# Staging the end of a second layer by a table of times, with a normalisation's division and weight in one VectorE product

## The chip, the cores and the metric

The kernel runs on one core of a Trainium2 chip. The metric is the device time of one execution in microseconds. The profiler has recorded one further execution; its times are those of the views below. Engines are named as in the profile: PE is TensorE, PEld its weight loads, DVE is VectorE, ACT is ScalarE, POOL is GpSimd, and SP issues the transfers.

## What is computed

The program is a network of four layers on an input of 2 x 56 x 56 tokens of 128 channels. The first two layers are scans in four directions, the third is an attention with a spectral mixer, the fourth an attention with experts. The change lies where the second layer ends and the third begins. For every token, the reference computes there (shortened):

```python
y = _layernorm(y, p['out_norm_w'], p['out_norm_b']) * jax.nn.silu(z)
out = y @ p['out_proj_w'].T                       # for each of four heads of 32 channels
prev = s + out + vss_skip * s                     # the head's block
x_res = cvm_skip * x_orig + jnp.concatenate(outs, axis=3)
x = _layernorm(x_res, final_ln_w, final_ln_b)     # 128 channels
u = _ln_t(x)                                      # a second normalisation, without weight
sim = jnp.einsum('blh,bmh->blm', u, u) * scale    # attention of the third layer
```

## The kernel before

The tokens lie as X, 112 partitions by 28 tiles by 2 images by 128 channels, in SBUF for the whole program. The stage between the last scan and attention 2 runs over seven chunks of four tiles (448 tokens) of both images together. A chunk goes through three bodies, called one after the other in a loop in `Layer1.run` (from L935):

- `after` (L872), for the last head: ScalarE squares y (L881), GpSimd multiplies y with the gate (L883), TensorE projects both and the mean of the squares (L888, L890, L892; the trace shows eight rows for each four matmuls), ScalarE takes the root (L894), VectorE its reciprocal (L895), `u` (L899), `t` (L903) and X (L905), and GpSimd adds to `u` between (L901).
- `last` (L910): the final layernorm of the second layer, in place in X. `layernorm_tokens` (L71) sums on VectorE (L78), scales (L79), subtracts (L80), squares on ScalarE (L81), sums (L82), takes root (L83, ScalarE) and reciprocal (L84), and then, as `last="ACT"`, scales each of the eight rows of 128 channels on ScalarE (L89). Two GpSimd passes over 112x1024 multiply with the weight and add the bias (both L918). Its tiles are called `stf` and `sqf`.
- `Attention2.chunk` (L1133): the second normalisation, of X into U, by the same function (tiles `stu` and `squ`). Then TensorE turns U (L1145), image by image; `evacuate` (L58) copies the result from PSUM to `uT`, a part of `big`, alternating between VectorE (L64) and ScalarE (L68); and `key_tiles` (L1279) turns `uT` back into tiles of keys (L1285), with one or two such copies.

Nothing in this loop fixes the order in which the instructions stand in the engines' queues. The framework's scheduler chooses it, from priorities and readiness, and it also places instructions of neighbouring parts among them: the small ones that form the mixer's weights (L1380 to L1409, L1707 to L1709), and the first score matmuls of attention 2 (L1076). The scans before it run inside `manual_schedule()`, where the order written is the order issued. In either case each engine works off its queue in that order, and an instruction waits until what it reads is there.

Behind the stage, `mixer_filters` clears a tile P (L1340), fills it by a transfer, and adds windows of it into D (L1349); attention 2 begins with scores (L1076) and their exponentials (L1078).

The pools decide how many chunks can be under way: `mid1` has two buffers for each of the tiles of `after` and `last`, `a2u` two for U, `squ` and `stu`, `pmid1` two PSUM tiles, `pa2` four.

Of the kernel before, what the change touches and what calls it, by code (L numbers as in the profile page):

```python
# [17 lines left out]
ALU = mybir.AluOpType  # L18
# [3 lines left out]
B = 2  # L22
HW = 56
L = HW * HW
C = 128
TP = 112
NT = L // TP
CH = 448
NCH = L // CH
# [38 lines left out]
            self.nc.scalar.copy(out, in_)  # L68


def layernorm_tokens(k, out, x, sq, st, d, by=None, last="POOL"):  # L71

    nc = k.nc
    g = x.shape[1]
    mean, var = st[:, 0, :], st[:, 1, :] if by is None else by
    nc.vector.tensor_reduce(mean, x, AX.X, ALU.add)  # L78
    nc.vector.tensor_scalar_mul(mean, mean, 1.0 / d)  # L79
    nc.vector.tensor_tensor(out, x, mean.unsqueeze(2).to_broadcast([TP, g, d]), ALU.subtract)  # L80
    nc.scalar.activation(sq, out, AF.Square)  # L81
    nc.vector.tensor_reduce(var, sq, AX.X, ALU.add)  # L82
    nc.scalar.activation(var, var, AF.Sqrt, bias=k.eps[:TP], scale=1.0 / d)  # L83
    nc.vector.reciprocal(var, var)  # L84
    if last == "POOL":
        nc.gpsimd.tensor_tensor(out, out, var.unsqueeze(2).to_broadcast([TP, g, d]), ALU.mult)
    else:
        for i in range(g):
            nc.scalar.activation(out[:, i], out[:, i], AF.Copy, scale=var[:, i : i + 1])  # L89


def tokens_to_channels(k, pool, dst, src):
# [18 lines left out]
class Scans:  # L111
# [190 lines left out]
    def run(self):  # L302
        with ExitStack() as ctx:
            self.open(ctx)
            with self.k.tc.manual_schedule():
                self.all_steps()
# [437 lines left out]
class Layer1:  # L744
# [79 lines left out]
    def chunk(self, t, c):  # L824
        return t[:, 4 * c : 4 * (c + 1)].rearrange("p j b c -> p (j b) c")
# [4 lines left out]
    def before(self, head, pools, c, pad):  # L830
# [5 lines left out]
        if c < NCH:  # L836
            sv = self.chunk(self.prev, c)
            xs = self.chunk(self.channels(head), c)
            if head == 0:
                nc.vector.tensor_copy(sv, xs)  # L840
            else:
                nc.vector.tensor_tensor(sv, sv, xs, ALU.add)
            nrm = sp.tile([TP, 4, B * D], F32, name="nrm")
            nv = nrm.rearrange("p j (b c) -> p (j b) c", c=D)
            sq = sp.tile([TP, 4 * B, D], F32, name="sq")
            st = sp.tile([TP, 2, 4 * B], F32, name="st")
            layernorm_tokens(k, nv, sv, sq, st, D)
            nc.gpsimd.tensor_scalar(xs, xs, self.R["cvm_skip"], None, ALU.mult)
            nc.gpsimd.tensor_scalar(sv, sv, self.R["vss_skip"], None, ALU.mult)
            pt = pp.tile([2 * D, CH], F32, name="pt")  # L850
            for i in range(4):
                nc.tensor.transpose(pt[:, TP * i : TP * (i + 1)], nrm[:, i], k.ident[:TP, :TP])
            nc.scalar.copy(self.hT[:, cs], pt)
            ps = vp.tile([128, CH], F32, name="pcv")
            nc.tensor.matmul(ps, lhsT=W["in_w"][:, 0, :], rhs=self.hT[:, cs], start=True, stop=True)
            nc.scalar.activation(
                pad[:, 1 + 8 * c : 9 + 8 * c, 1 : 1 + HW], ps.rearrange("p (r w) -> p r w", w=HW),
                AF.Identity, bias=self.inb[:, 0:1],
            )
# [10 lines left out]
            self.scans.first(vp)  # L870

    def after(self, head, pools, c):  # L872

        k, nc, D = self.k, self.k.nc, self.D
        sp, pp = pools
        cs = slice(CH * c, CH * (c + 1))
        y, gate = self.y[:, cs], self.z[:, cs]
        sq = sp.tile([128, CH], F32, name="sq0")  # L880
        nc.scalar.activation(sq, y, AF.Square)  # L881
        yz = sp.tile([128, CH], F32, name="yc0")
        nc.gpsimd.tensor_tensor(yz, y, gate, ALU.mult)  # L883
        p = pp.tile([TP, 2, 4, B * D], F32, name="p")
        pv = pp.tile([TP, 4 * B], F32, name="pv")
        tiles = [slice(TP * i, TP * (i + 1)) for i in range(4)]
        for i, ts in enumerate(tiles):
            nc.tensor.matmul(p[:, 1, i], lhsT=gate[:, ts], rhs=self.outs[1], start=True, stop=True)  # L888
        for i, ts in enumerate(tiles):
            nc.tensor.matmul(pv[:, B * i : B * (i + 1)], lhsT=sq[:, ts], rhs=self.mean, start=True, stop=True)  # L890
        for i, ts in enumerate(tiles):
            nc.tensor.matmul(p[:, 0, i], lhsT=yz[:, ts], rhs=self.outs[0], start=True, stop=True)  # L892
        rs = sp.tile([TP, 4 * B], F32, name="rs")
        nc.scalar.activation(rs, pv, AF.Sqrt, bias=k.eps[:TP])  # L894
        nc.vector.reciprocal(rs, rs)  # L895
        p1, p2 = (p[:, i].rearrange("p j (b c) -> p (j b) c", c=D) for i in range(2))
        s, x = self.chunk(self.prev, c), self.chunk(self.channels(head), c)
        u = sp.tile([TP, 4 * B, D], F32, name="u")
        nc.vector.tensor_tensor(u, p2, s, ALU.add)  # L899
        if head == 3:  # L900
            nc.gpsimd.tensor_tensor(u, u, x, ALU.add)  # L901
        t = sp.tile([TP, 4 * B, D], F32, name="t")
        nc.vector.tensor_tensor(t, p1, rs.unsqueeze(2).to_broadcast([TP, 4 * B, D]), ALU.mult)  # L903
        if head == 3:
            nc.vector.tensor_tensor(x, t, u, ALU.add)  # L905
        else:
            nc.vector.tensor_tensor(s, t, u, ALU.add)
            nc.gpsimd.tensor_tensor(x, x, s, ALU.add)

    def last(self, sp, c):  # L910

        k, nc = self.k, self.k.nc
        xv = self.chunk(k.X, c)
        sq = sp.tile([TP, 4 * B, C], F32, name="sqf")
        st = sp.tile([TP, 2, 4 * B], F32, name="stf")
        layernorm_tokens(k, xv, xv, sq, st, C, last="ACT")
        for op, n in ((ALU.mult, "final_ln_w"), (ALU.add, "final_ln_b")):
            nc.gpsimd.tensor_tensor(xv, xv, self.R[n].unsqueeze(1).to_broadcast([TP, 4 * B, C]), op)  # L918

    def opened(self, ctx):  # L920
        k, name = self.k, "mid1"
# [13 lines left out]
    def run(self, follow):  # L935


        k = self.k
        for head in range(1, 5):
            self.scans.run()  # L940
            with ExitStack() as ctx:
                pp = ctx.enter_context(k.pool("pmid1", 2, psum=True))
                if head < 4:
                    pad = self.opened(ctx)
                    sp = self.sp
                else:
                    sp = ctx.enter_context(k.pool("mid1", 2))
                    chunk = follow(ctx)
                for c in range(NCH + 1):
                    if c < NCH:  # L950
                        self.after(head - 1, (sp, pp), c)
                    if head < 4:
                        self.before(head, (sp, pp, self.vp), c, pad)
                    elif c < NCH:
                        self.last(sp, c)
                        chunk(c)

# [6 lines left out]
def bank(pool, name):  # L966
    return pool.tile([128, 512], F32, name=name)
# [150 lines left out]
class Attention2:  # L1118
# [14 lines left out]
    def chunk(self, c):  # L1133

        k, nc = self.k, self.k.nc
        U = self.sp.tile([TP, 4, B, C], F32, name="U")
        sq = self.sp.tile([TP, 4 * B, C], F32, name="squ")
        st = self.sp.tile([TP, 2, 4 * B], F32, name="stu")
        flat = "p j b c -> p (j b) c"
        x = k.X[:, 4 * c : 4 * (c + 1)].rearrange(flat)  # L1140
        layernorm_tokens(k, U.rearrange(flat), x, sq, st, C, last="ACT")
        for b in range(B):
            pt = bank(self.pp, "pt")[:, 0:CH]
            for i in range(4):
                nc.tensor.transpose(pt[:, TP * i : TP * (i + 1)], U[:, i, b, :], k.ident[:TP, :TP])  # L1145
            k.evacuate(self.uT[b][:, CH * c : CH * (c + 1)], pt)
            key_tiles(k, bank(self.pp, "pt"), self.uT[b], self.V[b], c)

    def run(self, early, inputs):
# [129 lines left out]
def key_tiles(k, ps, uT, V, c):  # L1279

    j0, j1 = CH * c // KT, NKT if c == NCH - 1 else CH * (c + 1) // KT
    ps = ps.rearrange("p (j c) -> p j c", c=C)
    for j in range(j0, j1):
        t = uT[:, KT * j : min(KT * (j + 1), L)]
        k.nc.tensor.transpose(ps[: t.shape[-1], j - j0, :], t, k.ident)  # L1285
    whole = min(j1, L // KT)
    k.evacuate(V[:, j0:whole], ps[:, 0 : whole - j0])
    if whole < j1:
        n = L - KT * whole
        k.evacuate(V[:n, whole], ps[:n, whole - j0])  # L1290
# [168 lines left out]
class Mixer:  # L1459
# [104 lines left out]
    def into(self, by, place, onto=None):  # L1564
# [3 lines left out]
        for outs in sorted(by, key=len):  # L1568
            ps = self.product(by[outs])
            for o in outs:  # L1570
# [4 lines left out]
                else:  # L1575
                    nc.vector.tensor_tensor(place(o), onto(o), ps, ALU.add)

    def unit(self, f0, eo, after, later, project):


# [463 lines left out]
```

## Time and profile before

| what | value |
|---|---|
| median of three runs | 9114.81 us (9106.39 to 9117.84) |
| the profiled execution | 9098.37 us |
| its span, first to last instruction | 9096.6 us |
| busy over the span: PE | 7993.2 us (88%) |
| busy over the span: DVE | 7088.0 us (78%) |
| busy over the span: POOL | 6350.1 us (70%) |
| busy over the span: ACT | 3854.8 us (42%) |
| mean granted TensorE clock | 0.951 |

The span is what the timeline's times count from. The busy shares are means over parts of the program with quite different limits; the stage of the change is about 120 us of the 9096.6. A row of the timeline gives the start, the time until its last instruction's end, engine, line, operation, what is written from what, the shape and how many instructions were merged; in brackets stands the engine's idle time before it and what ended that. Rows of the same stage by form give busy time and mean duration, then the idle time of the engine before them.

### The profile page before, as it was taken

The numbers are of one execution on the slowest core, as the hardware profiler recorded it, in microseconds if no ns is written. First come the engines' busy times: TensorE is split into PE (matmuls) and PEld (weight loads), VectorE is DVE, ScalarE is ACT, GpSimd is POOL, SyncE is SP. The second block draws the span as 40 slices with busy tenths as digits, with TensorE's granted clock in tenths as the row PEclk, the third lists the DMA queues.
The fourth block names the chain that finished last, engine by engine and source line by source line (L and its number), as shares of the span: only waits on it lengthen the run. The fifth ranks groups of instructions, "written<-read, shape, count | busy, mean of one in ns | idle before, by whom it ended". The sixth has DMA issues, their size and how long they took to land. (4 is left out here: it accounts for less than half of the span.)

```text
span 9096.6 us, 93496 instructions
## 1 busy us (share of the span) xinstructions
PE 7993.2 (88%) x28687; PEld 4765.5 (52%) x28687; DVE 7088.0 (78%) x7568; ACT 3854.8 (42%) x6644; POOL 6350.1 (70%) x4066
## 2 busy tenths in 40 slices
PE   8888888888887888888888888699999999999998
PEld 4444445444444444444444444355688888874555
DVE  8999998999997997998999899511467667665442
ACT  4555545555555555554554555433211111114331
POOL 6999996999996997998899799566311111115551
PEclk9999999999999998998999899799999999999999
DMA  5666664666664995996898699100233333320004
GB/s 159 221 221 220 222 212 127 221 221 220 222 220 110 230 226 134 227 228 157 203 227 204 157 227 224 39 3 3 85 96 105 104 94 110 93 63 8 14 1 135
DMA packets 780368, 1362.92 MB, mean 150 GB/s; under 512 B 133101, under 2 KB 405486, under 8 KB 779834
## 3 DMA queue, kind: packets, MB, share of 16 engines
q1 hardware_dynamic: 779866, 1356.95, 53.1%
q8 instruction: 227, 3.72, 0.2%
q14 instruction: 275, 2.25, 0.1%
HBM read 1317.03 MB, written 39.60 MB: 149 GB/s over the span
## 5 line engine op out<-in xcount | busy, mean ns | idle before, releaser
L430 POOL TENSOR_TENSOR p<-h,c 128x784 f32<-128x784 f32 x2048 | 3761.2, 1864 | 115.0 <-DVE h L358 33.1
L358 DVE TENSOR_TENSOR_SCAN h<-a,state,h 128x784 f32<-128x784 f32 x1536 | 2791.8, 1840 | 51.6 <-ACT a L339 28.7
L378 PE MATMUL acc<-p,center 128*128 128x392 f32 x4096 | 1499.0, 499 | 22.7 <-POOL p L430 20.8
L378 PE MATMUL acc<-p,ident 128*128 128x392 f32 x4096 | 1491.9, 498 | 6.7 <-POOL p L430 6.7
L417 DVE TENSOR_TENSOR h<-du,b 128x784 f32<-128x784 f32 x1408 | 1336.7, 949 | 75.6 <-PE b L364 70.4
L339 ACT ACTIVATE a<-delta,L0A 128x784 f32<-128x784 f32 x1024 | 939.3, 918 | 973.4 <-DVE h L358 971.5
L339 ACT ACTIVATE a<-delta,L1A 128x784 f32<-128x784 f32 x1024 | 939.2, 917 | 908.3 <-DVE h L358 905.3
L364 PE MATMUL b<-three,sel 96*128 96x512 bf16 (+1 forms) x2816 | 728.6, 341 | 563.9 <-DVE h L417 460.1
L433 POOL TENSOR_TENSOR h<-du,b 128x784 f32<-128x784 f32 x640 | 1190.3, 1860 | 4.1 <-PE pcv L460 4.1
L378 PEld LDWEIGHTS acc<-p,center 128*128 128x128 f32 x4096 | 740.9, 192 | 536.8 <-POOL p L430 60.2
L378 PEld LDWEIGHTS acc<-p,ident 128*128 128x128 f32 x4096 | 743.9, 192 | 512.8 <-POOL p L430 26.5
L1089 POOL TENSOR_TENSOR total<-total,e 128x448 f32<-128x448 f32 (+1 forms) x644 | 735.6, 1142 | 326.0 <-ACT e L1078 286.0
L358 DVE TENSOR_TENSOR_SCAN h<-a,h 128x784 f32<-128x784 f32 x512 | 901.7, 1780 | 36.7 <-ACT a L339 21.1
L364 PEld LDWEIGHTS <-sel 96*128 96x128 bf16 x2816 | 281.5, 100 | 1230.9 <-issue 1048.6
L1572 DVE TENSOR_TENSOR u<-u,cv 128x512 f32<-128x512 f32 x1024 | 623.7, 681 | 326.6 <-PE cv L1559 325.4
L1603 POOL TENSOR_TENSOR u<-u,S 128x1024 f32<-128x1024 f32 x64 | 150.0, 2365 | 1041.0 <-DVE S L1572 1041.0
L1078 ACT ACTIVATE e<-sc 128x448 f32<-128x448 f32 (+1 forms) x700 | 377.2, 543 | 723.0 <-PE sc L1076 596.3
L1574 ACT COPY u<-cv 128x512 f32<-128x512 f32 x256 | 149.5, 587 | 829.3 <-PE cv L1559 775.7
L1673 PE MATMUL pj<-u,Wm 128*128 128x196 f32 (+8 forms) x1536 | 354.7, 384 | 5.7 <-DVE A L1679 5.7
L1076 PE MATMUL sc<-big 128*128 128x448 f32 (+1 forms) x700 | 323.4, 547 | 15.4 <-ACT e L1078 12.3
L1070 PE MATMUL av<-e,big 128*128 128x448 f32 (+1 forms) x700 | 320.9, 545 | 1.2 <-DVE e L1083 1.0
L1653 POOL TENSOR_TENSOR both<-mpm 128x512 f32<-128x512 f32 x32 | 40.6, 1269 | 392.3 <-DVE Wm L1709 272.8
(452 smaller groups left out, 11251.1 us busy)
## 6 DMA issues: line engine op xcount, KB each, us to landing
c<-rows SPq DMA_DIRECT2D x1024, 392.0 KB, 4.0
c<-rows SPq DMA_DIRECT2D x2048, 196.0 KB, 4.8
b<-rows SPq DMA_DIRECT2D x320, 392.0 KB, 4.5
b<-rows SPq DMA_DIRECT2D x640, 196.0 KB, 4.6
H<-raw SPq DMA_DIRECT2D x32, 1568.0 KB, 7.6
wC<-win SPq DMA_DIRECT2D x64, 576.0 KB, 6.4
w<-in_L_weight_dram SPq DMA_DIRECT2D x52, 512.0 KB, 6.3
wA<-win SPq DMA_DIRECT2D x64, 384.0 KB, 5.6
```

What stands on the lines that cost most here:

```text
L339: self.k.nc.scalar.activation(x["a"], g["delta"][ci], AF.Exp, scale=self.w["A"](g["kd"], ci, x["n"]))
L358: self.k.nc.vector.tensor_tensor_scan(h, a, h, start, ALU.mult, ALU.add)
L364: self.k.nc.tensor.matmul(ps[:, c0:c1], lhsT=self.w["selB"](x["n"]), rhs=x["g"]["three"][:, c0:c1], start=True, stop=True)
L378: nc.tensor.matmul(job["acc"][:, i, 0:392], lhsT=self.w["sum"], rhs=x["p"][:, 392 * i : 392 * (i + 1)], start=False, stop=n == NS - 1,)
L417: nc.vector.tensor_tensor(one["h"], one["g"]["du"][one["ci"]], one["b"], ALU.mult)
L430: nc.gpsimd.tensor_tensor(now["p"], now["h"], now["c"], ALU.mult)
L433: nc.gpsimd.tensor_tensor(three["h"], three["g"]["du"][three["ci"]], three["b"], ALU.mult)
L1076: nc.tensor.matmul(ps[:n], lhsT=keys[b][:, KT * j : KT * j + n], rhs=q, start=True, stop=True)
L1078: nc.scalar.activation(e[:n], ps[:n], AF.Exp, scale=scale)
L1089: nc.gpsimd.tensor_tensor(total[:n], total[:n], e[:n], ALU.add)
L1572: nc.vector.tensor_tensor(place(o), place(o), ps, ALU.add)
L1673: nc.tensor.matmul(ps[:, lo - c0 : hi - c0], lhsT=Ws[f][:, eo, r, :], rhs=u[:, b, f, lo - a0 : hi - a0], start=f == 0, stop=f == 1,)
```

## The change

Functions become generators, which stop after some of their steps and say how many microseconds later their next step is due. `woven` runs several of them together: always the one whose next step is due first. The stage's chunks start 14.5 us apart in this reckoning, and the loop runs inside `manual_schedule()`. In the final layernorm, the eight scalings on ScalarE and the weight's pass on GpSimd give way to eight VectorE instructions, each of which multiplies with the reciprocal of the root and with the weight; the bias stays on GpSimd. In `chunk`, both images are turned and copied first, and the key tiles of both follow. All other callers of these functions run the generators through at once, and their instructions stand as before.

```diff
+def woven(stages, apart):
+    at = [(apart * i, i, one) for i, one in enumerate(stages)]
+    while at:
+        t, i, one = min(at, key=lambda a: a[:2])
+        at.remove((t, i, one))
+        wait = next(one, None)
+        if wait is not None:
+            at.append((t + wait, i, one))
 
-def layernorm_tokens(k, out, x, sq, st, d, by=None, last="POOL"):
+def layernorm_steps(k, out, x, sq, st, d, by=None, last="POOL", weight=None):
...
     nc.vector.tensor_tensor(out, x, mean.unsqueeze(2).to_broadcast([TP, g, d]), ALU.subtract)
+    yield 2.8
     nc.scalar.activation(sq, out, AF.Square)
+    yield 1.2
     nc.vector.tensor_reduce(var, sq, AX.X, ALU.add)
+    yield 1.4
     nc.scalar.activation(var, var, AF.Sqrt, bias=k.eps[:TP], scale=1.0 / d)
+    yield 0.5
     nc.vector.reciprocal(var, var)
-    if last == "POOL":
+    if weight is not None:
+        yield 0.1
+        for i in range(g):
+            nc.vector.scalar_tensor_tensor(out[:, i], out[:, i], var[:, i : i + 1], weight, ALU.mult, ALU.mult)
+        yield 2.4
+    elif last == "POOL":
         nc.gpsimd.tensor_tensor(out, out, var.unsqueeze(2).to_broadcast([TP, g, d]), ALU.mult)
     else:
+        yield 0.3
         for i in range(g):
             nc.scalar.activation(out[:, i], out[:, i], AF.Copy, scale=var[:, i : i + 1])
...
@@ after_steps @@
         for i, ts in enumerate(tiles):
             nc.tensor.matmul(p[:, 1, i], lhsT=gate[:, ts], rhs=self.outs[1], start=True, stop=True)
+        yield 1.6
...
             nc.tensor.matmul(p[:, 0, i], lhsT=yz[:, ts], rhs=self.outs[0], start=True, stop=True)
+        yield 1.8
         rs = sp.tile([TP, 4 * B], F32, name="rs")
...
             nc.gpsimd.tensor_tensor(u, u, x, ALU.add)
+        yield 1.7
...
@@ last_steps @@
-        layernorm_tokens(k, xv, xv, sq, st, C, last="ACT")
-        for op, n in ((ALU.mult, "final_ln_w"), (ALU.add, "final_ln_b")):
-            nc.gpsimd.tensor_tensor(xv, xv, self.R[n].unsqueeze(1).to_broadcast([TP, 4 * B, C]), op)
+        yield from layernorm_steps(k, xv, xv, sq, st, C, weight=self.R["final_ln_w"])
+        bias = self.R["final_ln_b"].unsqueeze(1).to_broadcast([TP, 4 * B, C])
+        nc.gpsimd.tensor_tensor(xv, xv, bias, ALU.add)
...
@@ Layer1.run @@
+                if head == 4:
+
+                    def end(c):
+                        yield from self.after_steps(3, (sp, pp), c)
+                        yield 0.9
+                        yield from self.last_steps(sp, c)
+                        yield 2.8
+                        yield from chunk(c)
+
+                    with k.tc.manual_schedule():
+                        woven((end(c) for c in range(NCH)), 14.5)
+                    continue
...
@@ Attention2.chunk @@
-        layernorm_tokens(k, U.rearrange(flat), x, sq, st, C, last="ACT")
+        yield from layernorm_steps(k, U.rearrange(flat), x, sq, st, C, last="ACT")
+        yield 1.5
         for b in range(B):
             pt = bank(self.pp, "pt")[:, 0:CH]
...
             k.evacuate(self.uT[b][:, CH * c : CH * (c + 1)], pt)
+        yield 3.0
+        for b in range(B):
             key_tiles(k, bank(self.pp, "pt"), self.uT[b], self.V[b], c)
```

More of the change, by code (lines that the diff above doesn't have):

```diff
@@ L68, in evacuate, with all_of @@
             self.nc.scalar.copy(out, in_)
-def layernorm_tokens(k, out, x, sq, st, d, by=None, last="POOL"):
+def all_of(steps):
+    for _ in steps:
+        pass
+def woven(stages, apart):
[7 more added lines that the diff above has]
+def layernorm_steps(k, out, x, sq, st, d, by=None, last="POOL", weight=None):
     nc = k.nc
@@ L80, in layernorm_tokens @@
     nc.vector.tensor_tensor(out, x, mean.unsqueeze(2).to_broadcast([TP, g, d]), ALU.subtract)
+    yield 2.8
     nc.scalar.activation(sq, out, AF.Square)
+    yield 1.2
     nc.vector.tensor_reduce(var, sq, AX.X, ALU.add)
+    yield 1.4
     nc.scalar.activation(var, var, AF.Sqrt, bias=k.eps[:TP], scale=1.0 / d)
+    yield 0.5
     nc.vector.reciprocal(var, var)
-    if last == "POOL":
+    if weight is not None:
[4 more added lines that the diff above has]
+    elif last == "POOL":
         nc.gpsimd.tensor_tensor(out, out, var.unsqueeze(2).to_broadcast([TP, g, d]), ALU.mult)
     else:
+        yield 0.3
         for i in range(g):
             nc.scalar.activation(out[:, i], out[:, i], AF.Copy, scale=var[:, i : i + 1])
+def layernorm_tokens(*args, **more):
+    all_of(layernorm_steps(*args, **more))
 def tokens_to_channels(k, pool, dst, src):
@@ L872, in after, with after_steps @@
     def after(self, head, pools, c):
+        all_of(self.after_steps(head, pools, c))
+    def after_steps(self, head, pools, c):
         k, nc, D = self.k, self.k.nc, self.D
@@ L908, in after, with last_steps @@
             nc.gpsimd.tensor_tensor(x, x, s, ALU.add)
-    def last(self, sp, c):
+    def last_steps(self, sp, c):
         k, nc = self.k, self.k.nc
@@ L951, in run @@
                         self.after(head - 1, (sp, pp), c)
[L952 to L956, printed above, removed]
+                    self.before(head, (sp, pp, self.vp), c, pad)
 KT = 128
```

## The prediction

> **What bounds the kernel now.** I read five views of the kernel before. The page first: its part 4, the chain that ended last, holds next to nothing in this profile (PE 0%, DVE 0%), so the stage has to be followed by hand. The slices show the place: in slice 26 of 40, between the scans and attention 2, the DMA rate falls from 224 to 39 GB/s and the granted TensorE clock is 7 tenths. Then the timeline from 5715 to 5865 us, for what starts and ends the stage:
>
> ```profile
> 5724.95 1.59 ACT L398 COPY big<-acc 128x392 f32<-128x392 f32 x2 [2.95 <-PE acc L378]
> ...
> 5756.51 1.22 DVE L80 TENSOR_TENSOR U<-X,stu 112x1024 f32<-112x1024 f32 x1
> ...
> 5834.06 1.23 DVE L80 TENSOR_TENSOR U<-X,stu 112x1024 f32<-112x1024 f32 x1
> ...
> 5844.15 1.51 POOL L1340 MEMSET P<- 32x1712 f32 x1 [11.98 <-PE pt L1145]
> ...
> 5848.72 1.75 DVE L1349 TENSOR_TENSOR D<-P 32x255 f32<-32x255 f32 x5 [2.30 <-DMA P<-in_L_phi_dram]
> ...
> 5856.21 1.28 ACT L1078 ACT_TABLE_LOAD   x1 [9.45 <-DVE D L1349]
> 5857.51 0.54 ACT L1078 ACTIVATE e<-sc 128x448 f32<-128x448 f32 x1
> ```
>
> The scans' last sums leave at 5724.95. The seven chunks' second normalisations (U, L80) start from 5756.51 to 5834.06, one per 77.55/6 = 12.9 us. The last transposes release the memset of P, 10.1 us after the last U starts; P's transfer, the chain that builds D and a table load then run one behind the other, and the first exponential of attention 2 waits for all of them. So what sets the end is the start of that memset, 5844.15: a microsecond there is a microsecond of the kernel.
>
> Next the busy time of the stretch (columns length, PE, PE weight load, VectorE, ScalarE, GpSimd, clock, DMA share, GB/s) and its waits:
>
> ```profile
> 5726.50:5847.00 120.50, 62.01 (x264) 48.14 (x264) 81.91 (x136) 65.97 (x174) 48.27 (x31) 0.54 0.01 1
> ...
> POOL X L918 <- ACT X L89: 35.3, 6, 10.1
> ...
> DVE stu L78 <- POOL X L918: 12.2, 4, 4.4
> ```
>
> No engine is full: VectorE, the busiest, works 82 of 120.5 us. The stage is bound by its chains of waits, through the ScalarE scalings (L89) and the two GpSimd passes (L918). Last, rows of one form, for durations:
>
> ```profile
> L89 ACT ACTIVATE X<-X,stf 112x128 f32<-112x128 f32 x56 | 18.2, 392 | 9.5 <-DVE stf L84 9.3
> L918 POOL TENSOR_TENSOR X<-X,L1final_ln_b 112x1024 f32<-112x1024 f32 x7 | 16.5, 2361 | 0.5
> L918 POOL TENSOR_TENSOR X<-X,L1final_ln_w 112x1024 f32<-112x1024 f32 x7 | 16.4, 2349 | 35.3 <-ACT X L89 35.3
> ...
> 5900.61 1.13 DVE L1115 SCALAR_TENSOR_TENSOR X<-pr,r,X 112x128 f32<-112x128 f32 x4
> ```
>
> **What the Trainium skill says.** "SBUF — State Buffer", section "Who interferes with whom": a VectorE instruction with two SBUF inputs and a GpSimd instruction that reads SBUF exclude each other for a whole instruction, while one with a single SBUF input doesn't contend. The trace agrees: X<-t,u (L905) takes 0.42 us alone and 2.55 us at 5749.98, when L918 held GpSimd from 5749.90; a reduction (L78) beside L918 stays at 1.21. "Perfetto Trace Analysis", section "Sequencer Loop": instructions go into an engine's queue in order and wait there for their semaphores. The timeline agrees: at 5777 to 5778.8 VectorE idles 2.41 us before L78 of U, for L918, with the later rows behind it.
>
> **The change, part by part.**
>
> *Product.* Per chunk it removes eight ScalarE scalings (x8 row, 2.45 us) and one GpSimd pass of 2.35 us, and adds eight VectorE products of 112x128. No row has this form with both inputs in SBUF. Bounds: below, L1115, same size with one input in PSUM, four in 1.13 us with 0.343 for one, so 0.262 apart; above, L1709's 0.485 for 256 elements with nothing overlapped. Eight give 7 x 0.262 + 0.343 = 2.18 us, or at most 3.9. I take 2.18: 256 to 384 elements in L1709 cost 0.485 to 0.617, 0.13 per 128, which puts a 128 at 0.35. One chunk's own chain gets 2.45 + 2.35 - 2.18 = 2.6 us shorter. VectorE's sum per chunk becomes: 1.43 (L895, L899, L903, L905) + 3.98 (L78, L79, L80, L82, L84) + 2.18 + 3.98 + 1.14 (two copies, L64) = 12.7 us.
>
> *Order.* The bodies of the chunks are now emitted in turns by a time table with 14.5 us between chunks, and nothing is reordered afterwards. SP issues the same transfers in the same order. The 14.5 is no clock: only the order in each queue counts. In the changed program, VectorE's queue from one bias to the next reads: L78, L79, L80 of U(c); rs, u, t, X(c+1); L78, L79, L80 of X(c+1); variance of U(c), its reciprocal; variance of X(c+1); copy of uT(c); reciprocal; eight products(c+1); copy of the keys(c); then L78 of U(c+1), which waits for bias(c+1). ScalarE's reads: rs(c+1) [done early], square U(c), root U(c), square X(c+1), eight scalings U(c), copy of uT(c), root X(c+1), copy, square of y(c+2). GpSimd's: bias(c), gated product(c+1), u(c+1), bias(c+1).
>
> Followed from the end of bias(c), with the trace's durations and 0.03 to 0.07 us from one engine to the next, as the timeline has them:
> - gated product L883 1.13, its eight matmul rows 1.70 (L892): 2.89. Beside it L78 1.22, L79 0.16, L80 1.14 and the reciprocal: 2.74, so the matmuls end last
> - u 0.42, GpSimd's u 0.72, X 0.43: 4.57
> - L78 1.21, L79 0.16, L80 1.14 of X(c+1): 7.18
> - variance of U(c) 1.21, which had been ready since 5 or so, behind the former: 8.39
> - root U(c), next after 0.20; square X(c+1), next after 0.95: 9.57
> - scalings of U(c): the seventh ends 6 x 0.295 + 0.387 = 2.16 later, then the last transpose of b = 0 and four of b = 1 (0.20 + 0.95): 12.92
> - ScalarE's copy, next after 0.44: 13.40; root X(c+1), which stood behind all this, 0.29: 13.72; reciprocal 0.20: 13.95
> - eight products 2.18: 16.2; bias(c+1) 2.36: 18.5
>
> So one turn takes 18.5 us, and hardly anything of the next turn goes on in it: the root of X(c+1) stands in ScalarE's queue behind U(c)'s scalings and a copy that waits for TensorE, and everything of chunk c+1 on VectorE stands behind L78 of U(c), which waits for the bias. VectorE is busy 12.7 of these 18.5.
>
> *Head.* The mixer's weights (L1386 to L1409, L1707 to L1709), now spread over the stage, go to its beginning: two table loads of 1.28 us stand before the first root, some 25 small VectorE instructions among the first chunk's. From 5726.6: square 0.48, table load, exp 0.2, table load, to 5729.9; root, u, X to 5732; mean and difference 2.7; square 1.1; variance behind two weight products 1.7; root and reciprocal 0.6, one more product 0.6, eight products 2.2, bias 2.4, L78 and L79 1.5: the first U at about 5745, 11.5 us earlier than before, since no other chunk stands in between.
>
> *Tail.* From the last U: 1.25 + 1.08 + 1.24 + 0.33 + 0.23, the seventh scaling 2.16, five transposes 1.19 and the handing over: 7.6 us to the memset (10.1 before, where its copies stood in the way).
>
> *Sum.* 5745 + 6 x 18.5 + 7.6 = 5863.6 to 5865 with the small gaps, against 5844.15: 20 us later. The small gaps are about 0.1 us a turn where a queue takes up an instruction with two waits. Everything behind (transfer, D, table load, attention) is the same chain. On the profiled execution, 9098.4 us (span 9096.6 and 1.8 around it), that gives 9118. This execution lies 16.4 us under the median of the runs, 9114.8; the difference belongs to no stage, so I put the 20 us on the median: 9135.
>
> **Rivals.**
> 1. *The busiest queue sets the pace* (not slower). If other chunks' work really covers each wait, the turn is VectorE's 12.7 us: 5745 + 76.2 + 7.6 = 5828.8, 15 us earlier, 9099; at the plan's 14.5 it is 4.5 earlier, 9110. It decides from a turn under (5844.15 - 7.6 - 5745)/6 = 15.2 us. For it: no engine is full, GpSimd and ScalarE lose 4.8 us per chunk. Against it: the queues' order above; 3.3 us of the loop would have to be wrong. 0.07, mostly within 0.2%.
> 2. *The port lock, or dear products.* L80 of U(c) starts some 0.3 us after GpSimd's product ends; if it comes first, or the products fall upon a GpSimd pass, a turn loses 1.1 to 2.35 us; products at 3.9 us cost 1.7. Six turns: 7 to 14 us more, 9142 to 9149. For it: 2.55 us at L905. Against it: the eight products end before the bias they release. 0.12.
> 3. *The later start is hidden.* If attention 2 waited for a transfer, the 20 us would vanish: 9115. Against it: 1 GB/s in the stage, and the wait is named, D. 0.05.
> That the order isn't what the change says can't be: the queues of the changed program have it.
>
> **How the numbers follow.** The forecast has 0.76. Its own error is about 0.5 us a turn, 3 us, and medians of such runs spread over 11 us (9106.4 to 9117.8), so 0.2%, 18.2 us, is about what a measurement can tell from no change, and 20 lies hardly above it: of the 0.76 I give 0.52 to slower and 0.24 to the same. With rival 2 slower, 3 the same, and 1 parted (0.02 faster, 0.05 same): faster 0.02, same 0.34, slower 0.64. The range: 6 us below the forecast for an error of 1 us a turn, and as much for the runs, 9121; above, rival 2 to its end, 9150.
>
> **What would show it.** U starts 18 to 19 us apart; VectorE idle before L78 of stu, for the bias, in every chunk, some 1.5 to 2 us; ScalarE's root of stf 4 to 5 us after square sqf ended; eight products in 2.2 us; the memset of P at about 5864. U starts 15 us apart or less make it wrong, and so do turns of 20 or more with GpSimd rows longer than 2.4 us.

## The result and the profile after

The changed kernel takes 9124.4 us (median of 16 runs, 9115.64 to 9135.65). In the same series the kernel before takes 9107.1 (16 runs, 9091.74 to 9117.84). The ratio of the changed kernel to the one before, worked out from these runs, is 1.0021, with a 95% interval of 1.0015 to 1.0028: 19 us slower, between 14 and 26; the two medians are 17.3 us apart. The forecast was 20 us more than before.

The profiled execution of the changed kernel is a long one, 9135.65 us, with a span of 9133.9; its span is 37.3 us longer than that of before. The timeline says how much of this is the change. Below are the timeline's rows at the ends of the stage, in the kernel after:

```profile
5733.43 1.59 ACT L430 COPY big<-acc 128x392 f32<-128x392 f32 x2 [2.78 <-PE acc L410]
...
5753.81 1.23 DVE L98 TENSOR_TENSOR U<-X,stu 112x1024 f32<-112x1024 f32 x1
...
5866.23 1.23 DVE L98 TENSOR_TENSOR U<-X,stu 112x1024 f32<-112x1024 f32 x1
...
5873.92 1.51 POOL L1389 MEMSET P<- 32x1712 f32 x1 [9.18 <-PE pt L1192]
...
5887.20 0.54 ACT L1124 ACTIVATE e<-sc 128x448 f32<-128x448 f32 x1
```

The stage begins 8.48 us later than before, in scans that the change doesn't touch. From there to the memset of P it is 140.49 us long, against 5844.15 - 5724.95 = 119.20 before: 21.3 more. From the memset to the first exponential it is 13.28, against 13.36. Behind that, the rest of the span is 7.6 us longer than before. On both sides of the stage the engines have the same instructions in the same order. So 21.3 of the 37.3 us are the stage, and the other 16.0 are the spread between executions. Times of whole runs spread over some 20 us; the stage's length in the trace is free of what lies outside it, so the experiments are read by it: the stage from the copy of the scans' last sums to the memset of P, in one trace of each kernel.

In the changed kernel the lines have other numbers. A normalisation is L96 (sum), L97 (scaling of the sums), L98 (subtraction), L100 (square), L102 (sum of the squares), L104 (root) and L106 (reciprocal), and behind it come the eight products (L110) or ScalarE's eight scalings (L117). L956 is the bias, L918 the gated product and L928 its projection, L936 `u`, L938 GpSimd's addition to `u`, L943 X; L1192 are the transposes of U and L1334 the key tiles. The tiles tell the two normalisations apart: `stf` and `sqf` belong to the final layernorm, `stu` and `squ` to the second.

One turn of the stage, in the kernel after, from the timeline (TensorE's rows and a few others left out):

```profile
5787.58 2.34 POOL L956 TENSOR_TENSOR X<-X,L1final_ln_b 112x1024 f32<-112x1024 f32 x1 [12.26 <-DVE X L110]
...
5789.95 1.22 DVE L96 TENSOR_REDUCE stu<-X 112x8 f32<-112x1024 f32 x1 [1.92 <-POOL X L956]
...
5793.43 0.73 POOL L938 TENSOR_TENSOR u<-u,X 112x256 f32<-112x256 f32 x1 [2.41 <-DVE u L936]
5794.18 0.43 DVE L943 TENSOR_TENSOR X<-t,u 112x256 f32<-112x256 f32 x1 [0.57 <-POOL u L938]
...
5797.25 1.21 DVE L102 TENSOR_REDUCE stu<-squ 112x8 f32<-112x1024 f32 x1
5798.49 0.30 ACT L104 ACTIVATE stu<-stu,eps 112x8 f32<-112x8 f32 x1 [4.76 <-DVE stu L102]
5798.70 1.04 ACT L100 ACTIVATE sqf<-X 112x1024 f32<-112x1024 f32 x1
...
5799.65 2.43 ACT L117 ACTIVATE U<-U,stu 112x128 f32<-112x128 f32 x8
...
5803.07 0.53 ACT L68 COPY big<-pt 128x448 f32<-128x448 f32 x1 [0.99 <-PE pt L1192]
5803.50 0.30 ACT L104 ACTIVATE stf<-stf,eps 112x8 f32<-112x8 f32 x1
5803.84 0.20 DVE L106 RECIPROCAL stf<-stf 112x8 f32<-112x8 f32 x1 [0.89 <-ACT stf L104]
5804.08 2.19 DVE L110 SCALAR_TENSOR_TENSOR X<-X,stf,L1final_ln_w 112x128 f32<-112x128 f32 x8
...
5806.41 2.35 POOL L956 TENSOR_TENSOR X<-X,L1final_ln_b 112x1024 f32<-112x1024 f32 x1 [12.26 <-DVE X L110]
```

From bias to bias it is 18.83 us. The loop is all there: the bias of chunk c releases the mean of U(c); behind it on VectorE stand u, X and the mean of chunk c+1, then the variance of U(c); that releases ScalarE's root, its square of X(c+1) and its scalings of U(c); the root of X(c+1) stands behind those and behind a copy that TensorE has to release; then come reciprocal, products and the bias of c+1. GpSimd idles 12.26 us before the bias in all turns but the last. Over the stage, VectorE is busy 92.5 of 140.5 us and no engine more.

That this copy stands in ScalarE's queue comes from the edit in `chunk`. `evacuate` goes to the other engine at each call. Before, the key tiles followed each image, and VectorE made 13 of the 14 copies of `uT`; with the key tiles of both images moved behind, it makes the first image's and ScalarE the second's (7 each). No run puts that copy back on VectorE at 14.5 us.

### The profile page after: what moved, and what is told of

Its sections match the earlier page's. It is cut to its first block, busy times and chain, and to the rows that moved or that the text cites. A ratio compares the mean times of both kernels' runs of the same rounds, so it can differ in the third digit from the quotient of the medians.

```text
span 9133.9 us, 93486 instructions
## 1 busy us (share of the span) xinstructions
PE 8008.4 (88%) x28687; PEld 4777.4 (52%) x28687; DVE 7099.4 (78%) x7624; ACT 3839.2 (42%) x6588; POOL 6328.6 (69%) x4059
```

## The experiments

Stage and turns are from the traces. A turn is the mean distance of the starts of U. Ratios are against the kernel before, from runs on the same chip; a dash where the kernel ran only once. First U counts from the start of the stage.

| kernel | stage us | turn us | first U | ratio |
|---|---|---|---|---|
| before | 119.20 | 12.9 | 31.6 | |
| after | 140.49 | 18.74 | 20.4 | 1.0021 (1.0015 to 1.0028) |
| product alone | 117.76 | 13.1 | 28.7 | 0.9996 (0.9988 to 1.0005) |
| order alone | 162.53 | 21.9 | 23.6 | 1.0045 (1.0031 to 1.0059) |
| 6.5 apart | 109.61 | 12.4 | 26.7 | 0.9989 (0.9982 to 0.9995) |
| 6.5 apart, copies on ScalarE | 107.27 | 12.1 | 26.8 | 0.9991 (0.9984 to 0.9997) |
| after, extra sum in the idle time | 140.95 | 18.81 | 20.4 | - |
| after, extra sum in the loop | 147.72 | 19.94 | 20.4 | - |
| after, 2.8 ahead of the scalings | 131.95 | 17.3 | 20.4 | 1.0018 (1.0010 to 1.0025) |
| after, 3.1 ahead of the scalings | 145.71 | 19.6 | 20.4 | - |
| 6.5 apart, no product | 113.10 | 13.2 | 25.6 | 0.9994 (0.9985 to 1.0003) |
| 7.0 apart | 125.66 | 14.9 | 27.2 | - |

### The two halves of the change, each alone

Product alone: the generators run one after another, and the scheduler orders them.

```diff
-                    with k.tc.manual_schedule():
-                        woven((end(c) for c in range(NCH)), 14.5)
+                    for c in range(NCH):
+                        all_of(end(c))
                     continue
...
             k.evacuate(self.uT[b][:, CH * c : CH * (c + 1)], pt)
-        yield 3.0
-        for b in range(B):
             key_tiles(k, bank(self.pp, "pt"), self.uT[b], self.V[b], c)
```

> The weight's product on VectorE, but the loop as it was before: chunk after chunk, order left to the scheduler. Stage length here and below: from the copy of the scans' last sums to the memset of P, 119.2 us before, 140.5 after. Theory (the order written by hand is the cause, the product is good by itself): 2.6 us of each chunk's chain are gone, most of it hidden behind other chunks, so the stage is 115 to 118 us, the kernel 1 to 4 us faster than before. Rival (the product burdens VectorE, the busiest engine of the stage, with 2.2 us a chunk): 125 us or more, the kernel 6 us or more slower.

Order alone: the weave stays, the final layernorm is the old one.

```diff
-        yield from layernorm_steps(k, xv, xv, sq, st, C, weight=self.R["final_ln_w"])
-        bias = self.R["final_ln_b"].unsqueeze(1).to_broadcast([TP, 4 * B, C])
-        nc.gpsimd.tensor_tensor(xv, xv, bias, ALU.add)
+        yield from layernorm_steps(k, xv, xv, sq, st, C, last="ACT")
+        yield 2.4
+        for op, n in ((ALU.mult, "final_ln_w"), (ALU.add, "final_ln_b")):
+            nc.gpsimd.tensor_tensor(xv, xv, self.R[n].unsqueeze(1).to_broadcast([TP, 4 * B, C]), op)
```

> The order by times with 14.5 us between chunks, but eight scalings on ScalarE and two GpSimd passes as before. Theory (a loop through two chunks): the turn gets 2.45 + 2.35 - 2.18 and the hand-over longer, plus a wait of ScalarE's queue, 21.3 to 22.2 us; stage 156 to 164 us, kernel 36 to 45 us slower than before. Rival (the product is what costs): turn below 18.7 us, stage below 140.

The product alone gives a stage of 117.76 us, 1.4 less than before; in whole runs that is too small to be seen, and the forecast of 1 to 4 us stays open there. The order alone gives 162.53, with turns of 22.03 to 22.06 us between all chunks but the last two; stage, turns and whole runs (41 us slower) lie within what was expected. So the loss is the order's. Within this order the product is worth 162.53 - 140.49 = 22.0 us; within the scheduler's, 1.4.

### Is it a loop, or an engine's work?

The same extra VectorE instruction, a sum over a constant of 112x1024 into a tile that nobody reads, stands once where VectorE waits for the bias and once in the chain that I take for the loop.

```diff
+        more = self.sp.tile([TP, 4 * B], F32, name="more")
+        one = k.ident[:TP].unsqueeze(1).to_broadcast([TP, 4 * B, C])
+        nc.vector.tensor_reduce(more, one, AX.X, ALU.add)
         yield from layernorm_steps(k, U.rearrange(flat), x, sq, st, C, last="ACT")
```

> The changed kernel with one more VectorE sum per chunk (constant of 112x1024 into a scratch tile, 1.2 us), placed just ahead of the mean of U, where VectorE waits for the bias some 1.9 us. Theory (loop of waits): free; turns stay 18.7 us, the wait for the bias shrinks to 0.8, stage 140.5 us within 0.5. Rival (VectorE's work sets the pace): turns 19.9, stage 148 to 149.

```diff
+        also = lambda: nc.vector.tensor_reduce(more, one, AX.X, ALU.add)
-        yield from layernorm_steps(k, U.rearrange(flat), x, sq, st, C, last="ACT")
+        yield from layernorm_steps(k, U.rearrange(flat), x, sq, st, C, last="ACT", also=also)
...
     yield 1.2
+    also()
     nc.vector.tensor_reduce(var, sq, AX.X, ALU.add)
```

> The same extra sum, placed ahead of the variance of U, a link of the loop. Theory: every turn 1.14 us longer, 19.9 us; stage 147 to 149 us. Rival (some other engine sets the pace): stage stays at 140.5.

The timeline of the first of these, around the wait (in the second run, L103 and L957 are L102 and L956 of after):

```profile
5788.55 1.21 DVE L1189 TENSOR_REDUCE more<-ident 112x8 f32<-112x1024 f32 x1
5790.55 1.22 DVE L96 TENSOR_REDUCE stu<-X 112x8 f32<-112x1024 f32 x1 [0.80 <-POOL X L956]
```

and of the second:

```profile
5797.32 1.22 DVE L96 TENSOR_REDUCE stu<-X 112x8 f32<-112x1024 f32 x1 [1.92 <-POOL X L957]
...
5804.61 1.21 DVE L1190 TENSOR_REDUCE more<-ident 112x8 f32<-112x1024 f32 x1
5805.74 1.21 DVE L103 TENSOR_REDUCE stu<-squ 112x8 f32<-112x1024 f32 x1
```

In the idle time the sum is free: the wait for the bias falls from 1.92 to 0.80 us and the turns stay (18.81, with 18.83 between the middle chunks as in after). In the loop every turn is 1.12 us longer (19.95 between the middle chunks), and the wait is 1.92 as it was. The same work on the same engine, at no cost in one place and at its full price in the other: the turn is the length of a chain and not the load of VectorE.

### Opening the loop at one point

The number ahead of ScalarE's scalings goes from 0.3 to 2.8, so that they are emitted after the next chunk's root:

```diff
     else:
-        yield 0.3
+        yield 2.8
         for i in range(g):
             nc.scalar.activation(out[:, i], out[:, i], AF.Copy, scale=var[:, i : i + 1])
```

> The changed kernel with one number changed: 2.8 in place of 0.3 ahead of ScalarE's eight scalings, which puts the next chunk's root and reciprocal ahead of this chunk's scalings, transposes and copies. Theory (the root's place in ScalarE's queue closes the loop): the piece from scalings to copy, 3.8 us, leaves the loop, a wait for the variance takes part of it back: turns of 16 to 17.3 us, stage 125 to 132 us, kernel 8 to 15 us faster than after. Rival (the loop is closed elsewhere, by TensorE's transposes or the copies): turns 18 us or more, stage 136 or more.

Its timeline:

```profile
5792.51 2.43 ACT L117 ACTIVATE U<-U,stu 112x128 f32<-112x128 f32 x8
...
5794.84 0.28 ACT L104 ACTIVATE stf<-stf,eps 112x8 f32<-112x8 f32 x1
...
5795.40 2.19 DVE L110 SCALAR_TENSOR_TENSOR X<-X,stf,L1final_ln_w 112x128 f32<-112x128 f32 x8
```

The turn is 17.3 us and the stage 131.95, 8.5 us less than after; both lie at the slow end of what was expected. In whole runs the gain over after doesn't show: the two ratios differ by 0.0003, some 3 us, where 8 to 15 were expected, and their intervals overlap, so that 8.5 us are neither seen nor ruled out. And the edit did not do what the expectation says: the scalings still stand ahead of the root. By the table both were due at 25.9 us (14.5 + 11.4 for the one, 23.1 + 2.8 for the other), and on a tie the earlier chunk goes first. The root moved only past the transposes and the copy, from 3.85 us behind the scalings' start (5799.65 to 5803.50 in after) to 2.33 (5792.51 to 5794.84): 1.5 us of the turn. So the place of the root does cost, but this run doesn't show what it costs to have it first. The next one does, with 3.1:

> 3.1 in place of 2.8 ahead of ScalarE's scalings: at 2.8 they and the next chunk's root were due at the same 25.9 us and the earlier chunk's went first; at 3.1 the root really stands first. Theory (a turn is the longest loop through the queues, whatever stands in it): the bias of c+1 starts earlier, but the copies and key tiles of U(c) slip behind; TensorE's key tiles now stand behind a projection that waits for the gated product, which waits for the bias, and on VectorE the copy of the keys stands ahead of the next mean. A new loop closes: turns near 20.3 us, stage 143 to 148 us, longer than after. Rival (each thing taken out of the first loop shortens the turn): turns of 15.5 to 16.5, stage 121 to 127 us.

```profile
5804.15 0.30 ACT L104 ACTIVATE stf<-stf,eps 112x8 f32<-112x8 f32 x1 [1.29 <-DVE stf L102]
5804.36 2.43 ACT L117 ACTIVATE U<-U,stu 112x128 f32<-112x128 f32 x8
...
5807.06 2.35 POOL L956 TENSOR_TENSOR X<-X,L1final_ln_b 112x1024 f32<-112x1024 f32 x1 [9.78 <-PE pt L1192]
...
5809.36 1.13 POOL L918 TENSOR_TENSOR yc<-big,pair 128x448 f32<-128x448 f32 x1
5810.54 1.76 PE L928 MATMUL p<-outonw,yc 128*112 128x64 f32 x8
5812.09 1.49 PE L1334 MATMUL pt<-ident,big 128*128 128x128 f32 x6
5812.98 0.56 DVE L64 COPY big<-pt 128x384 f32<-128x384 f32 x1 [5.32 <-PE pt L1334]
5813.45 1.21 DVE L96 TENSOR_REDUCE stu<-X 112x8 f32<-112x1024 f32 x1
```

Now the root stands first, and the bias starts 2.70 us after the scalings (6.76 in after). But the turns are 20.1 to 20.5 us, except for the last with 16.2, and the stage is 145.71, as expected. The bias ends at 5809.41, and the mean that it releases starts only at 5813.45: ahead of it on VectorE stands the copy of the keys, which waits 5.32 us for TensorE's key tiles (L1334), and these stand behind the projection (L928) of a gated product that GpSimd makes after the bias. With 2.8 a turn takes 17.3 us and with 3.1 it takes 20.3: what left the first loop came into another.

### Another distance, another order

> The changed kernel with 6.5 in place of 14.5: a third chunk is in the mix, and in the queues the instructions of one chunk's second normalisation stand behind those of a later chunk's first in other places. Theory (the order alone decides, the number is no clock): turns of 13 to 13.5 us, VectorE's sum of 12.7 nearly full; first U some 7 us later than after; stage 109 to 112 us, kernel 8 to 11 us faster than before. Rival (chunks nearer to each other only press the same engines harder): stage 135 us or more.

```diff
-                        woven((end(c) for c in range(NCH)), 14.5)
+                        woven((end(c) for c in range(NCH)), 6.5)
```

The next kernel has this too, and in addition, in `Attention2.chunk`:

```diff
-            k.evacuate(self.uT[b][:, CH * c : CH * (c + 1)], pt)
+            nc.scalar.copy(self.uT[b][:, CH * c : CH * (c + 1)], pt)
```

> As with 6.5 between chunks, and both copies of the turned U on ScalarE in place of one on each engine: VectorE's sum per chunk falls by 0.55 us. Theory (VectorE is the bound once the order is good): turns of 12.9 to 13.3, stage 107 to 110 us. Rival (still the chain of waits, now with two copies one behind the other): no shorter than with 6.5 alone, or up to 3 us longer.

The busy times of the stage in the kernel with both copies on ScalarE (columns as in the prediction):

```profile
5734.88:5842.15 107.27, 58.74 (x265) 47.65 (x266) 92.99 (x183) 53.67 (x124) 29.45 (x24) 0.55 0.00 1
```

With 6.5 the stage is 109.61 us and with the copies 107.27: VectorE is busy 93 of 107 us there, and its two longest waits lie at the ends, 5.0 us at the head for the mixer's exponential and 4.5 for the last key tiles, begun inside the stage. Both stages lie within what was expected. Both kernels beat the one before as well as the one after: the ratios' intervals end at 0.9995 and 0.9997. The two are not told apart by whole runs; in the trace the copies save 2.3 us.

The same distance without the product, with the final layernorm as in the order alone:

> 6.5 between the chunks, with the eight ScalarE scalings and both GpSimd passes as before, so without the product. Theory (the order does nearly all): stage 111 to 114 us, that is 2 to 4 us more than with the product at 6.5. Rival (a good order is only possible because the product frees ScalarE and GpSimd): stage 119 us or more.

It takes 113.10, 3.5 us more than with the product and still 6.1 less than before. The other way round, the product alone gains 1.4 us and the order on top of it 8.2. So the better part of the gain over before is the order's. In whole runs this kernel can't be told from the one before (0.9985 to 1.0003).

And with 7.0 in place of 6.5, nothing else:

> The changed kernel with 7.0 in place of 14.5. Theory (the number acts only through the order that falls out of it, by jumps): half a microsecond more than in the good one closes a loop again; turns near 17 us, stage 127 to 131 us. Rival (the distance acts smoothly): stage 108 to 112 us, as with 6.5.

Half a microsecond more in the table costs 16.1 us: 125.66, 1.3 us below the range that was expected. Middle turns are 16.6, near the expected 17 and 3 longer than at 6.5. The number has no smooth effect; it picks an order. But the reason given, a loop that closes again, is not what the trace shows:

```profile
5777.05 3.26 DVE L110 SCALAR_TENSOR_TENSOR X<-X,stf,L1final_ln_w 112x128 f32<-112x128 f32 x8
5777.20 1.13 POOL L918 TENSOR_TENSOR yc<-big,pair 128x448 f32<-128x448 f32 x1
...
5780.46 2.35 POOL L956 TENSOR_TENSOR X<-X,L1final_ln_b 112x1024 f32<-112x1024 f32 x1 [2.13 <-DVE X L110]
5780.76 2.33 DVE L943 TENSOR_TENSOR X<-t,u 112x256 f32<-112x256 f32 x1
```

The eight products take 3.26 us beside a gated product on GpSimd, against 2.19 in after, and X takes 2.33 us beside the bias, against 0.43. This is the port lock of rival 2, 3.0 us in a turn, where at 6.5 it takes 1.2 (shown at the end). From U to U, VectorE is busy 15.13 of 16.55 us here (5774.75 to 5791.30, 24 instructions), and 12.97 of 13.27 us at 6.5 (5767.51 to 5780.78, 25 instructions). So 2.2 of the 3.3 us more are busy time of VectorE, of which the lock makes up 1.8, and the other 1.1 are waits.

## Why the prediction was right, by its steps

- *What sets the end:* right. The memset of P came 21.3 us later after the scans' end, and the first exponential with it; the time from the one to the other changed by 0.08 us. Rival 3, a hidden shift, is out.
- *Product:* eight in 2.18 to 2.19 us, as taken (2.18), with 0.344 for one. Both inputs in SBUF cost no more than one in PSUM. In the changed kernel no product met a GpSimd pass (343 to 353 ns over all 56), and GpSimd's bias stayed at 2.34: rival 2 is out for this kernel. It came true at 7.0 between the chunks.
- *Order:* the turn was put at 18.5 us and came out at 18.74 on average, 18.83 between the middle chunks. The links are those of the list: u starts 2.93 us after the bias's end (2.89 there), the scalings 9.73 (9.57), and from the scalings' start to the next bias it is 6.76 (6.61). Of the 0.3 us a turn that are missing, about 0.2 lie in the two hand-overs from VectorE to GpSimd (`u` to GpSimd's addition, products to bias). They take 0.14 to 0.16 us each in the middle turns; the prediction took 0.03 to 0.07 for every hand-over. The kernel before showed it already: from TensorE's projection (L892) to GpSimd's next gated product (L883) it was 0.15.
- *Head:* first U 20.4 us after the copy of the scans' sums; forecast 20 (5745 against 5724.95).
- *Tail:* 7.69, forecast 7.6.
- *Rival 1*, the busiest queue as the pace, is out for the changed kernel: the extra sum in the idle time cost nothing. It came true in another order: at 6.5, the turns are 12.9 to 13.45 but for the last, and VectorE is busy 12.97 us in one of 13.27. So the rival's reason, that no engine was full, was sound; it wanted an order that lets the queue run.
- *The sum:* 20 against 21.3 in the stage, and 19 (14 to 26) in whole runs. Head, turns and tail are each a little short, so no error hides another. The time itself came out 10.6 us below the 9135 forecast, since before's median fell from 9114.8 to 9107.1 over more runs, 7.7 us; the other 2.9 are the difference between 20, rounded up in 9135, and the 17.3 between the medians.
- *A reading* is off, without consequence: VectorE's wait of 2.41 us before L78 of U at 5778.80 begins at 5776.4, not at 5777.

The change joins a good half to a bad one. The product takes 2.6 us from a chunk's chain by the prediction's sum. The weave, by where it puts instructions in two queues, ties the chains of two neighbouring chunks into one.

## What to carry to other kernels

An order written by hand is as good as its longest loop. Write down each engine's queue over one period, follow it from an instruction back to its successor one period later, and add up: if the loop is longer than the busiest engine's work, the queue has to be changed, and no faster instruction off the loop helps. The busiest engine's work is no constant either: where an order puts VectorE's instructions with two SBUF inputs beside GpSimd's passes, they get longer, by 3.0 us a turn at 7.0 and not at all in after. A table of due times that leaves out how long engines are taken gives an order by accident: half a microsecond in it was worth 16 in the stage, 0.3 was worth 14.

## What the runs showed that was not expected

At 6.5 us apart, the scaling of eight sums per partition (L97), a VectorE instruction with one input, was held up by GpSimd's bias for over a microsecond. Rows of that line in the kernel with 6.5 (count, then minimum, median and maximum in ns), and the timeline there:

```profile
L97 DVE TENSOR_SCALAR stf<-stf x7: 170/1350/1361, 5737.7 to 5813.8; 112x8 f32<-112x8 f32 x7
L97 DVE TENSOR_SCALAR stu<-stu x7: 170/171/172, 5754.4 to 5828.8; 112x8 f32<-112x8 f32 x7
```

```profile
5772.21 1.21 DVE L96 TENSOR_REDUCE stf<-X 112x8 f32<-112x1024 f32 x1
5772.44 2.35 POOL L956 TENSOR_TENSOR X<-X,L1final_ln_b 112x1024 f32<-112x1024 f32 x1 [5.53 <-DVE X L110]
5773.46 1.35 DVE L97 TENSOR_SCALAR stf<-stf 112x8 f32<-112x8 f32 x1
5774.85 1.22 DVE L98 TENSOR_TENSOR X<-X,stf 112x1024 f32<-112x1024 f32 x1
```

The scaling ends at 5774.81, the bias at 5774.79; the sum ahead of it ran beside the bias at its usual 1.21. Fifteen of these scalings in four kernels began during a bias pass (product alone 2, 6.5 apart 6, both copies on ScalarE 6, 7.0 apart 1); each ended 0.02 to 0.04 us after it. The Trainium skill's page "SBUF — State Buffer", section "Who interferes with whom", says that `tensor_scalar` can enter a mode that takes the port pair shared with GpSimd, and can then contend with it, when its operands meet that mode's conditions, while a reduction never contends on Trainium2. These rows agree, and show it for as few as eight elements per partition. It would probably not help to move the next instruction, L98, ahead: it has two SBUF inputs, like the sum into X, which was held in the kernel before (L905, 2.55 us) and at 7.0 (L943, 2.33 us). What might help was not tried: VectorE work with one PSUM input in that place.
